# Decoder with causal self-attention on one core: the projections of a slot run ahead of a visit's transpositions instead of behind them

## The chip, the core and the metric

The kernel runs on one core of a Trainium2 chip. A core has TensorE (matmuls and transposes, results in PSUM), VectorE, ScalarE and GpSimd, which work on SBUF, and SyncE, which issues the DMAs here. Each engine takes its own instructions in order; semaphores tie them together. In the profile they are PE (with PEld for its weight loads), DVE, ACT, POOL and SP. The metric is the device time of one execution in microseconds: median 2737.55 us of three runs before the change (2737.44 to 2737.64).

## The reference

A small encoder works on a context of 2 x 77 rows of 512 numbers, and a decoder on 2 x 2048 rows of 512, everything in float32, 16 heads of 32. The part that matters here is the decoder's causal self-attention:

```python
yn = _ln(y, dec_n1_s, dec_n1_b)
q = yn @ wq.T + bq;  k = yn @ wk.T + bk;  v = yn @ wv.T + bv     # 16 heads of 32
scores = einsum('bhqd,bhkd->bhqk', q, k) / sqrt(32) + rel_bias + causal
out = einsum('bhqk,bhkd->bhqd', softmax(scores), v)
y = y + out @ w_out.T + b_out
y = y + _mha(_ln(y, dec_n2_s, dec_n2_b), memory, ...)            # 77 keys of the encoder
y = y + relu(_ln(y, ...) @ ff1.T + b1) @ ff2.T + b2
```

The relative bias is constant beyond a distance of 128, so that only the last two blocks of 128 keys of a row of blocks need a table added; the others need none, after the table has been shifted by its constant.

## The kernel before, in words

The self-attention is cut into units (b, m, g, t): batch b of 2, block m of 512 rows (4 of them), group g of four heads (4), tile t of 128 query rows (4). There are 128 units, taken in this order. Unit (b, m, g, t) attends to i + 1 blocks of 128 keys, with i = 4 m + t. The key blocks are cut into pieces of up to four (`pieces`), and one round of the main loop (a visit) handles up to two pieces of a unit. Blocks m = 0 and m = 1 have one visit per unit, m = 2 and m = 3 two: the last visit of a unit is the one with `ends` true.

A unit goes through these steps. `scores` (L375): for each piece four matmuls on TensorE, one head each, into four PSUM banks; VectorE takes them to the SBUF buffer `pp` and keeps the maxima (L384 for the far blocks, L391 for the last two with their table), and after the last piece forms the negated maximum (L401). Four exponentials on ScalarE (L406, one for each head, held in the list `late_exps` and issued by `exps`) work in place in `pp`. `turn` (L426): each 128 x 128 block is transposed by TensorE, four transposes to a bank, and each bank is copied to one of eight buffers `pts`, by ScalarE (L433) or VectorE (L431). For m = 0 a bank holds the blocks of one head and the two engines alternate; for m > 0 a bank holds one key block of the four heads and the first half of the copies is ScalarE's, the later half VectorE's (with eight banks VectorE has the fifth and the seventh). `turn` issues one exponential after its fourth bank (after the eighth of eight) and up to four at its end. `values` (L455): values times transposed probabilities, four heads at a time, into one bank, which is copied to `oT` (L466, L468, L470).

Scores run two units ahead: `may_score` lets a piece of unit n be scored as soon as unit n - 2 has turned the blocks that lie in the same part of `pp`.

PSUM has eight banks, handed out in turn by `bank()` from the list `ring`; a bank is used again after seven others, and its next matmul waits until the copy out of it has been made. `values` takes a bank out of the ring while it sums.

Beside the units there is a `slot` for each: stages of other work, put down by hand in three lists by number of slot. `light` stages come first (normalising rows of later blocks with `norm_turn`, L305 and L310; dividing by the sums with `spread`; loads of bias tables; cross-attention of an earlier block), then the jobs with weights: `q_job` (L215), `k_job` (L226), `v_job` (L239) for the next blocks, the seven-product `part_job` (L1068), each with one or two banks and a copy out of it by VectorE or ScalarE. The `late` stages follow, among them the stages of the encoder (L577 to L820, its scores at L606 with VectorE work at L615 and L616). Slot n + 1 is issued in the last visit of unit n.

After the units a second part computes cross-attention and feed-forward for the remaining blocks; the change does not touch it. The schedule is by hand: each engine runs its instructions in the order in which the program calls them.

Of the kernel before, what the change touches and what calls it, by code (L numbers as in the profile page):

```python
# [54 lines left out]
def tile_encoder_decoder(ctx: ExitStack, tc: tile.TileContext, ins, out):  # L55
# [103 lines left out]
    with (  # L159
# [20 lines left out]
        def bank():  # L180

            ring.append(ring.pop(0))
            return psum[:, ring[-1], :]

        def in_turn(what, tile):
            i = count[what] % tile.shape[1]
            count[what] += 1
            return tile[:, i, :]
# [140 lines left out]
        units = [(b, m, g, t) for b in range(B) for m in range(NMB) for g in range(NC) for t in range(TB)]  # L329
# [22 lines left out]
        def exps(k):  # L352

            for _ in range(min(k, len(late_exps))):
                late_exps.pop(0)[1]()
# [56 lines left out]
        def turn(pieces):  # L412

            first = units[pieces[0][0]][1] == 0
            loads = []
            for n, k0, kn in pieces:
                ks = range(k0, k0 + kn)
                if first:
                    loads += [[(n, k, r) for k in ks] for r in range(HC)]
                else:  # L420
                    loads += [[(n, k, r) for r in range(HC)] for k in ks]
            for o, load in enumerate(loads):
                pt = bank()
                pts = in_turn("pts", pts_all).rearrange("p (x q) -> p x q", q=P)
                for x, (n, k, r) in enumerate(load):
                    nc.tensor.transpose(pt[:, ts(x, P)], state[n]["p"][r][:, k], ident)  # L426
                    got[n, k, r] = pts[:, x, :]
                w = len(load) * P
                free = pieces[0][0] == len(units) - 2 and pieces[0][1]
                if free or (o % 2 if first else o in (4, 6) if len(loads) == 8 else o >= (len(loads) + 1) // 2):  # L430
                    nc.vector.tensor_copy(pts[:, : len(load), :], pt[:, :w])  # L431
                else:
                    nc.scalar.copy(pts[:, : len(load), :], pt[:, :w])  # L433
                if not first and o == (7 if len(loads) == 8 else min(3, len(loads) - 1)):
                    exps(1)
            exps(HC if first else 0 if units[pieces[0][0]][1] == NMB - 1 else 1)
# [3 lines left out]
        def values(pair):  # L440
            n, k0, _ = pair[0]
            b, m, g, t = units[n]
            i = m * TB + t
            k1 = pair[-1][1] + pair[-1][2]
            whole = m == 0
            key = (b, m, g) if whole else n
            begun = key in sums_held
            if not begun:
                sums_held[key] = ring.pop(0)
            v = sums_held[key]  # L450
            ot = psum[:, v, ts(t, P)] if whole else psum[:, v, :P]
            keep = t < TB - 1 if whole else (g, t) == (2, 0) and k1 <= i
            for k in range(k0, k1):
                for r in range(HC):
                    nc.tensor.matmul(  # L455
                        ot[rows4(r)], vv[:, k, ts(g * HC + r, HD)], got.pop((n, k, r)),
                        start=k == k0 and (whole or not begun), stop=k == k1 - 1 and (whole or not keep),
                    )
            if keep:
                return  # L460
            if (b, m, g) not in ots:
                ots_at[b, m, g] = count["oT"] % oT_all.shape[1]
                ots[b, m, g] = in_turn("oT", oT_all)
            o = ots[b, m, g]
            if whole:
                nc.scalar.copy(o, psum[:, v, :])  # L466
            elif k0 == 0 or begun:
                nc.scalar.copy(o[:, ts(t, P)], ot)  # L468
            else:
                nc.vector.tensor_tensor(o[:, ts(t, P)], ot, o[:, ts(t, P)], ALU.add)  # L470
            ring.append(sums_held.pop(key))
# [644 lines left out]
        for x, (b, m) in enumerate(blocks):  # L1116
# [28 lines left out]
            for t in range(TB):  # L1145
                end = x == len(blocks) - 1
# [44 lines left out]
        def load_next():  # L1191

            while len(loaded) < min(len(queue), ran[0] + (5 if ran[0] < 4 else 4)):
                ahead = [queue[i][2] for i in range(ran[0], len(loaded) + 1)]
                if sum(ahead) > 3:
                    break
                loaded.append(queue[len(loaded)][0]())
# [45 lines left out]
        def slot(n):  # L1243
            for f in light[n]:
                f()
            for _, run, _ in jobs[n]:
                load_next()
                run(loaded[ran[0]])
                ran[0] += 1
            for f in late[n]:  # L1250
                f()
            if n == 5:
                load_next()
# [205 lines left out]
        def feed(upto):  # L1459
            while fed[0] < upto:  # L1460
                src = next(tiles, None)
                if src is None:
                    return
                dst = w_ring[fed[0] % len(w_ring)]
                fed[0] += 1
                if len(src.shape) == 3:
                    dst = dst.rearrange("p (c o) -> p c o", c=2)
                nc.sync.dma_start(dst, src)
# [302 lines left out]
        end = len(units)  # L1771
# [3 lines left out]
        def may_score():  # L1775

            if at[0] == len(stream):
                return False
            n, k0, kn = stream[at[0]]
            if n < 2:  # L1780
                return True
            moved = TB * max(0, units[n - 2][1] - units[n][1]) if n % 2 else 0
            return turned_to[n - 2] >= min(k0 + kn + moved, size[n - 2])

        def score_next():
            n, k0, kn = stream[at[0]]
            scores(n, k0, kn)
            scored_to[n] = k0 + kn
            at[0] += 1

        def score_two():

            n, k0, kn = stream[at[0]]
            at[0] += 1
            both = may_score()
            at[0] -= 1
            if both and stream[at[0] + 1][0] == n and stream[at[0] + 1][2] < kn:
                scores(*stream[at[0] + 1])
                scores(n, k0, kn)
                scored_to[n] = size[n]  # L1800
                at[0] += 2
            else:
                score_next()
                if both:
                    score_next()
# [5 lines left out]
        while i < len(stream):  # L1811
            n = stream[i][0]
            pair = [p for p in stream[i : i + 2] if p[0] == n]
            while scored_to.get(n) != size[n]:
                score_next()
            while any(u == n for u, _ in late_exps):
                exps(1)
            ends = pair[-1][1] + pair[-1][2] == size[n]
            turn(pair)
            if n == end - 2:  # L1820
                for _, k0, _ in pair:
                    feed(k0 + 4)
            turned_to[n] = pair[-1][1] + pair[-1][2]
            third = units[n][1] == 2
            if third and ends:
                exps(2)
            if ends and n + 1 < end:
                slot(n + 1)
            if not third:
                exps((0, 2, 1, 1)[units[n][1]])  # L1830
            if may_score():
                if len(pair) > 1 and units[n][1]:
                    score_two()
                else:
                    score_next()
            values(pair)
            while may_score() and (len(pair) > 1 or units[n][1] == 0):
                score_next()
            if third and not ends:
                exps(2)  # L1840
            i += len(pair)
# [68 lines left out]
```

## Time and profile before

| what | value |
|---|---|
| median of three runs | 2737.55 us |
| the profiled execution: own time, span | 2739.13 us, 2737.3 us |
| PE busy | 2711.1 us (99%) |
| DVE busy | 1821.8 us (67%) |
| ACT busy | 1539.9 us (56%) |
| POOL busy | 991.1 us (36%) |
| L426, transposes of probabilities, on PE | 527.6 us, 4352 instructions |
| L375, scores, on PE | 331.7 us, 2560 instructions |
| L455, values, on PE | 278.8 us, 8704 instructions |
| L431, copies of transposed blocks by DVE | 251.6 us, 404 instructions |
| L433, the same by ACT | 383.6 us, 732 instructions |

A row of the timeline gives start and duration in us from the span's start, engine, line, operation, written and read buffers, shape and the number of instructions that were merged into it; in brackets stands the idle time before it and what ended it. Score and value matmuls are recorded twice each, so a scored piece shows eight records. Ends of matmuls are modelled, so that the distance between starts says more than the durations. The units run from about 28 us to 1663 us of the span.

### The profile page before, as it was taken

The page shows a single profiled execution, that of the slowest core. Times are in us where ns is not written, and L with a number is a line of the kernel's source. Part 1 is how long each engine was busy: PE and PEld are TensorE (multiplying, and loading weights), DVE is VectorE, ACT ScalarE, POOL GpSimd, SP SyncE. Part 2 cuts the span into 40 slices and gives each one's busy share as a digit, 9 for nine tenths or more (in the row PEclk, how much of TensorE's full clock was granted, in tenths as well). Part 3 has the DMA queues.
Part 4 walks back from the last instruction along what each step waited for, and adds up shares of the span by engine and source line. Part 5 has one row for each costly group of instructions (what it writes and reads, how often), then busy time and mean ns, then how long its engine had stood idle before and what let it go on. Part 6 is the DMA issues. An engine that isn't in the chain of part 4 may idle for free.

```text
span 2737.3 us, 67718 instructions
## 1 busy us (share of the span) xinstructions
PE 2711.1 (99%) x26462; PEld 2182.6 (80%) x26462; DVE 1821.8 (67%) x5338; ACT 1539.9 (56%) x2996; POOL 991.1 (36%) x836
## 2 busy tenths in 40 slices
PE   9999999999999999999999999999999999999998
PEld 5578777777776677777777887898989898989898
DVE  5776687787875587687787793646464746464645
ACT  3554567767786557667777785444444444444431
POOL 1512234500210513313300103465646564646456
PEclk9999999999999999999999999999999999999999
DMA  7624345511212522333311206565758565756465
GB/s 225 182 86 133 121 126 176 161 55 41 63 48 72 147 75 71 108 111 106 128 44 33 64 19 225 166 220 166 219 166 242 165 219 166 220 166 220 150 224 185
DMA packets 293666, 377.47 MB, mean 138 GB/s; under 512 B 39984, under 2 KB 163936, under 8 KB 293218
## 3 DMA queue, kind: packets, MB, share of 16 engines
q1 hardware_dynamic: 293346, 373.12, 44.3%
q8 instruction: 210, 3.44, 0.5%
q14 instruction: 110, 0.90, 0.1%
HBM read 328.38 MB, written 44.64 MB: 136 GB/s over the span
## 4 chain that ended last, share of the span: by engine, by line
PE 94%; ACT 2%; DVE 2%; issue 1%; POOL 0%; DMA 0%; SPq 0%; ACTq 0%; DVEq 0%; POOLq 0%
PE psum L426 18%; PE psum L1556 14%; PE psum L1585 12%; PE psum L375 11%; PE psum L455 9%; PE psum L1068 8%; PE psum L215 4%; PE psum L1719 3%; PE psum L1676 3%; PE psum L865 2%; ACT pp L406 1%; PE psum L835 1%; PE psum L873 1%; PE psum L589 1%; PE psum L810 1%; PE psum L239 1%
## 5 line engine op out<-in xcount | busy, mean ns | idle before, releaser
L406 ACT ACTIVATE pp<-pp,nm 128x128 f32<-128x128 f32 (+15 forms) x512 | 611.9, 1201 | 30.1 <-DVE nm L401 29.6
L384 DVE TENSOR_SCALAR_CACHE_REDUCE pp<-psum 128x512 f32<-128x512 f32 (+3 forms) x1024 | 556.4, 591 | 56.2 <-PE psum L375 53.7
L433 ACT COPY pts<-psum 128x512 f32<-128x512 f32 (+2 forms) x732 | 383.6, 580 | 277.0 <-PE psum L426 224.8
L426 PE MATMUL psum<-ident,pp 128*128 128x128 f32 x4352 | 527.6, 276 | 9.7 <-ACT nT L310 4.5
L426 PEld LDWEIGHTS psum<-ident,pp 128*128 128x128 f32 x4352 | 471.4, 140 | 67.1 <-DVE pp L384 24.0
L375 PE MATMUL psum<-kT,q 32*128 32x512 f32 (+3 forms) x2560 | 331.7, 560 | 2.8 <-ACT nT L310 1.6
L455 PEld LDWEIGHTS psum<-pts,vv 128*32 128x32 f32 x8704 | 226.6, 110 | 126.5 <-DVE pp L384 47.0
L431 DVE COPY pts<-psum 128x512 f32<-128x512 f32 (+3 forms) x404 | 251.6, 654 | 94.5 <-PE psum L426 92.5
L1585 PE MATMUL psum<-pp 128*128 128x128 f32 x2560 | 304.5, 276 | 1.9 <-POOL pp L961 1.6
L1585 PEld LDWEIGHTS psum<-pp 128*128 128x128 f32 x2560 | 296.3, 192 | 8.6 <-issue 3.0
L455 PE MATMUL psum<-pts,vv 128*32 128x128 f32 x8704 | 278.8, 275 | 0.7 <-DVE mx L391 0.3
L961 POOL TENSOR_TENSOR pp<-pp 128x512 f32<-128x512 f32 x159 | 212.9, 1356 | 121.0 <-DMA pp<-in_dec_ff_wT_dram 45.4
L1556 PE MATMUL psum<-vv,pp 128*128 128x256 f32 x1024 | 236.2, 381 | 0.0
L375 PEld LDWEIGHTS psum<-kT,q 32*128 32x128 f32 x2560 | 142.1, 183 | 106.7 <-issue 42.0
L1556 PEld LDWEIGHTS psum<-vv,pp 128*128 128x128 f32 x1024 | 190.3, 190 | 25.8 <-issue 0.5
L391 DVE CUSTOM_DVE_ANT_0 pp<-psum,bias 128x256 f32<-128x256 f32 (+1 forms) x512 | 196.0, 411 | 20.9 <-PE psum L375 20.8
L1569 DVE TENSOR_TENSOR kT<-kT,psum 128x512 f32<-128x512 f32 x96 | 65.8, 686 | 191.1 <-PE psum L1556 190.9
L1572 ACT ACTIVATE kT<-kT,vecs 128x256 f32<-128x256 f32 x192 | 87.1, 501 | 156.6 <-DVE kT L1569 155.9
L1556 PE MATMUL psum<-nT,pp 128*128 128x256 f32 x768 | 174.1, 380 | 0.0
L1556 PEld LDWEIGHTS psum<-nT,pp 128*128 128x128 f32 x768 | 144.2, 190 | 20.3 <-issue 1.6
L1593 ACT COPY oT<-psum 128x128 f32<-128x128 f32 x56 | 15.0, 268 | 238.8 <-PE psum L1585 238.8
L493 POOL TENSOR_TENSOR oT<-rirows,oT 128x512 f32<-128x512 f32 x30 | 38.4, 1279 | 288.5 <-DMA rirows<-rec 239.9
(257 smaller groups left out, 4049.3 us busy)
## 6 DMA issues: line engine op xcount, KB each, us to landing
pp<-w_d SPq DMA_DIRECT2D x520, 256.0 KB
pp<-in_dec_ff_wT_dram SPq DMA_DIRECT2D x112, 256.0 KB
wqk<-in_dec_sa_in_wT_dram SPq DMA_DIRECT2D x76, 256.0 KB
bias<-tzg SPq DMA_DIRECT2D x128, 128.0 KB
pp<-wo_d SPq DMA_DIRECT2D x56, 256.0 KB
vv<-in_enc_ff_wT_dram SPq DMA_DIRECT2D x8, 1024.0 KB
xr<-in_x_dram SPq DMA_DIRECT2D x32, 256.0 KB
vv<-y SPq DMA_DIRECT2D x32, 256.0 KB
```

Source lines behind the costliest of these rows:

```text
L375: nc.tensor.matmul(banks[r][:, : kn * P], q[rows4(r), ts(t, P)], kT[rows4(r), g, k0 * P : (k0 + kn) * P], start=True, stop=True,)
L384: nc.vector.tensor_scalar(p[:, k0 : k0 + far], s[:, :far], 1.0, None, ALU.mult, ALU.max, accum_out=st["mx"][:, r, c : c + 1],)
L391: nc.vector.tensor_tensor_reduce(p[:, k0 + far : i + 1], s[:, far:kn], near[:, 2 - (kn - far) :], 1.0, LOWEST, ALU.add, ALU.max, accum_out ...
L406: nc.scalar.activation(p, p, AF.Exp, bias=nm, accum_out=to)
L426: nc.tensor.transpose(pt[:, ts(x, P)], state[n]["p"][r][:, k], ident)
L431: nc.vector.tensor_copy(pts[:, : len(load), :], pt[:, :w])
L433: nc.scalar.copy(pts[:, : len(load), :], pt[:, :w])
L455: nc.tensor.matmul(ot[rows4(r)], vv[:, k, ts(g * HC + r, HD)], got.pop((n, k, r)), start=k == k0 and (whole or not begun), stop=k == k1 - ...
L961: engine.tensor_tensor(out, a, b, ALU.subtract)
L1068: nc.tensor.matmul(mm[:, ts(f, TOK)], left[:, c, ts(f, P)], right[:, c, :], start=c == 0, stop=c == 1,)
L1556: nc.tensor.matmul(mm[:, ts(f, TOK)], a[:, c, ts(f, P)], b[:, c, :], start=fresh and f == 0 and c == 0, stop=c == 1, skip_group_check=True,)
L1585: nc.tensor.matmul(psum[:, bank_i, ts(col, P)], lhs[:, c, :], w[:, c, :], start=fresh and k in (0, 3) and c == 0, stop=c == 3, skip_group_ ...
```

## The change

The call of `slot(n + 1)` in a unit's last visit moves from behind `turn` to ahead of it, and with it, for m = 2, the issue of up to two exponentials. The order in a last visit was: transpose, slot, scores, values. It is now: slot, transpose, scores, values. So a slot's work stands between the values of the visit before and the transpositions. Nothing is added or left out. Visits that do not end a unit stay as they are.

```diff
             ends = pair[-1][1] + pair[-1][2] == size[n]
+            third = units[n][1] == 2
+            if ends and n + 1 < end:
+                if third:
+                    exps(2)
+                slot(n + 1)
             turn(pair)
             if n == end - 2:
                 for _, k0, _ in pair:
                     feed(k0 + 4)
             turned_to[n] = pair[-1][1] + pair[-1][2]
-            third = units[n][1] == 2
-            if third and ends:
-                exps(2)
-            if ends and n + 1 < end:
-                slot(n + 1)
             if not third:
                 exps((0, 2, 1, 1)[units[n][1]])
             if may_score():
```

## The prediction

> **What bounds the kernel now.** I read the page's busy shares and chain of waits first, then TensorE's timeline visit by visit, then VectorE's and ScalarE's timelines beside it. The page settles the engine.
>
> ```profile
> PE 2711.1 (99%) x26462; PEld 2182.6 (80%) x26462; DVE 1821.8 (67%) x5338; ACT 1539.9 (56%) x2996; POOL 991.1 (36%) x836
> PE 94%; ACT 2%; DVE 2%; issue 1%; POOL 0%; DMA 0%; SPq 0%; ACTq 0%; DVEq 0%; POOLq 0%
> ```
>
> TensorE is at work for 2711.1 of 2737.3 us and carries 94% of the chain. Its work is not changed by the edit: the same matmuls run in another order. So the time can move only through stalls of TensorE, and many of these are hidden in "busy", because the ends of matmuls are modelled. I take a stall as the distance from the start of one group to the start of the next, less the same distance where nothing stalls. In this way four kinds of group are told apart in a visit: T (transposes of probabilities, L426), J (the slot's jobs, here L215), S (scores, L375) and V (values, L455).
>
> The first fence is TensorE's timeline in the last quarter of a batch (m = 3), two units whose last visit has a slot with one projection. The second is the same part of two later units whose slot holds no matmul, so that S follows T at once, which is what the change makes of every last visit.
>
> ```profile
> 619.17 2.84 PE L426 MATMUL psum<-ident,pp 128*128 128x128 f32 x24
> 621.84 3.60 PE L215 MATMUL psum<-nT,wqk 128*128 128x512 f32 x8
> 625.37 2.03 PE L375 MATMUL psum<-kT,q 32*128 32x512 f32 x16
> 627.34 1.52 PE L455 MATMUL psum<-pts,vv 128*32 128x128 f32 x48
> 628.78 4.18 PE L426 MATMUL psum<-ident,pp 128*128 128x128 f32 x32
> 632.90 2.00 PE L375 MATMUL psum<-kT,q 32*128 32x512 f32 x16
> ...
> 672.63 2.40 PE L426 MATMUL psum<-ident,pp 128*128 128x128 f32 x20
> 674.87 3.60 PE L215 MATMUL psum<-nT,wqk 128*128 128x512 f32 x8
> 678.40 2.04 PE L375 MATMUL psum<-kT,q 32*128 32x384 f32 x16
> 680.36 1.30 PE L455 MATMUL psum<-pts,vv 128*32 128x128 f32 x40
> ...
> 685.24 1.14 PE L375 MATMUL psum<-kT,q 32*128 32x512 f32 x8
> ```
>
> ```profile
> 812.16 2.40 PE L426 MATMUL psum<-ident,pp 128*128 128x128 f32 x20
> ...
> 821.66 2.00 PE L375 MATMUL psum<-kT,q 32*128 32x512 f32 x16
> ...
> 825.48 2.84 PE L426 MATMUL psum<-ident,pp 128*128 128x128 f32 x24
> 828.25 2.53 PE L375 MATMUL psum<-kT,q 32*128 32x512 f32 x16
> 830.70 1.52 PE L455 MATMUL psum<-pts,vv 128*32 128x128 f32 x48
> 832.15 3.79 PE L426 MATMUL psum<-ident,pp 128*128 128x128 f32 x32
> 835.87 0.50 PE L375 MATMUL psum<-kT,q 32*128 32x128 f32 x8
> ```
>
> The reader is to see two things. A projection costs 3.53 us (621.84 to 625.37) wherever it stands. And S straight behind T takes 2.45 us (828.25 to 830.70) against 1.97 (625.37 to 627.34) behind a projection: 0.48 more. But the next T is then quicker, 3.72 (832.15 to 835.87) against 4.12 (628.78 to 632.90), so most of it comes back.
>
> **The change part by part.** *The order on TensorE.* In a unit's last visit T, J, S, V becomes J, T, S, V. Of the 128 units 127 have such a slot. Each sequence has the same matmuls, so the first cost is nothing; what covers the copies of T's banks to SBUF changes. Before, J runs while VectorE and ScalarE empty the banks; after, S must be given banks that T has just filled, and V must read the last copy, with S alone between. What is queued behind a waiting S is all of TensorE: V, the next J, the next T.
>
> *Price of S behind T, blocks m = 1 and 3.* From the first T of the last visit to the S of the next visit, less the slot's 3.53: 632.90 - 619.17 - 3.53 = 10.20 with a slot and 835.87 - 825.48 = 10.39 without, +0.19; for the 20 transposes 685.24 - 672.63 - 3.53 = 9.08 and 821.66 - 812.16 = 9.50, +0.42. The cause is on VectorE, in the same stretch:
>
> ```profile
> 827.10 0.69 DVE L384 TENSOR_SCALAR_CACHE_REDUCE pp<-psum 128x512 f32<-128x512 f32 x1
> 827.72 1.88 DVE L431 COPY pts<-psum 128x512 f32<-128x512 f32 x3
> ```
>
> VectorE still empties the scores of the visit before when T ends its fourth load, and its three copies finish at 829.60, 4.12 us after T began. With J ahead of T it has had 3.53 us more and is through. The fourth load (16 of 24 transposes, 2.77 x 16/24 = 1.85 us after T's start) then starts the copies at once: they finish 1.85 + 1.88 = 3.73 us after T's start, 0.39 earlier. So I take 0.1 us a visit, half of the smaller price, with bounds 0 and 0.42. It applies to 49 visits: 30 of the 32 of m = 1 and 19 of the 32 of m = 3 have matmul work for a microsecond or two in their slot. 49 x 0.1 = +5 us, bounds 0 and +21.
>
> *m = 2.* The last visit turns two to four blocks (one to two VectorE copies) and scores one piece into four banks that T did not use. No such wait is to be seen; 0. The two exponentials that the edit puts ahead of the slot find an empty list, since the visit before has issued all four.
>
> *Slots with hardly any matmul.* In eight last visits of m = 1, 2, 3 the slot is a normalised tile's four transposes, alone or with a short stage of cross-attention.
>
> ```profile
> 747.63 0.60 PE L305 MATMUL psum<-ident,xt 128*128 128x128 f32 x4
> 748.16 1.93 PE L375 MATMUL psum<-kT,q 32*128 32x384 f32 x12
> 750.92 1.13 PE L375 MATMUL psum<-kT,q 32*128 32x512 f32 x4 [0.83 <-ACT nT L310]
> 751.98 1.30 PE L455 MATMUL psum<-pts,vv 128*32 128x128 f32 x40
> ```
>
> ```profile
> 747.57 1.81 ACT L406 ACTIVATE pp<-pp,nm 128x1792 f32<-128x1792 f32 x1
> 749.35 1.51 ACT L310 ACTIVATE nT<-psum,vecs 128x128 f32<-128x128 f32 x4
> ```
>
> S takes 3.82 here (748.16 to 751.98) instead of 1.96 (678.40 to 680.36), since its last bank is the slot's, which ScalarE empties behind T's copies and an exponential. After the change the slot's four activations come first on ScalarE, ahead of T's copies. If all eight lose this 1.86 now, 15 us could be had. But those activations then delay T's copies and both exponentials by 1.51, and ScalarE has no less to do; I take half, -7, bounds -15 and 0.
>
> *m = 0.* A visit here is short, and VectorE copies T's second and fourth bank.
>
> ```profile
> 81.56 0.52 PE L426 MATMUL psum<-ident,pp 128*128 128x128 f32 x3 [0.57 <-ACT pts L433]
> 82.15 3.70 PE L226 MATMUL psum<-nT,wqk 128*128 128x512 f32 x8
> ...
> 87.26 0.50 PE L375 MATMUL psum<-kT,q 32*128 32x128 f32 x8 [0.69 <-ACT kT L231]
> 87.69 0.86 PE L455 MATMUL psum<-pts,vv 128*32 128x128 f32 x24
> ```
>
> ```profile
> 77.63 1.63 DVE L615 TENSOR_TENSOR pp<-psum,pp 77x308 f32<-77x308 f32 x4
> 79.29 1.43 DVE L616 TENSOR_REDUCE emx<-pp 77x16 f32<-77x1232 f32 x1
> ...
> 83.59 1.01 DVE L431 COPY pts<-psum 128x384 f32<-128x384 f32 x2
> ```
>
> ```profile
> 108.20 1.20 PE L426 MATMUL psum<-ident,pp 128*128 128x128 f32 x9 [1.41 <-ACT nT L310]
> ...
> 113.90 1.53 PE L426 MATMUL psum<-ident,pp 128*128 128x128 f32 x12 [1.81 <-ACT nT L310]
> ```
>
> With 12 or 16 transposes S lasts 0.43 (87.26 to 87.69) or little more, and one VectorE copy is 1.01 / 2 = 0.51: V now waits some 0.25 us in the 16 visits with t of 2 or 3, +4. The encoder's scores hold VectorE from 77.63 to 80.72. Before, J's 3.7 us at 82.15 hide that T's copies come only at 83.59; after, in the two slots with encoder scores, T's copies stand right behind 3.1 us of this work, while T and S last 1.4 + 0.43: about 2 us of wait each, +4, less the waits of 0.57 and 0.69 and a long S that stand there now, so +2. Against it: T waits 1.41 and 1.81 for a bank that the slot before filled; a slot directly ahead of T, and S and V between the next pair, shift this; half of it, and as much for waits of T on VectorE behind the last scores, which then have a projection's time: -3.5. m = 0 together +2.5, bounds -3 and +8.
>
> *Other queues.* GpSimd's instructions keep their order. SyncE's differ in one place, the last unit: three loads go ahead of ten weight tiles for the feed-forward part.
>
> ```profile
> 1412.00:1663.00 251.00, 249.78 (x3356) 197.42 (x3356) 200.13 (x654) 196.52 (x293) 22.59 (x18) 1.00 0.19 61
> ```
>
> The last column but one is the share of the DMA engines, 0.19 there, with matmuls of several microseconds between issue and use: 0. Were the cover gone, one tile's delay would cost a wait of its landing at most once. Elsewhere each slot's loads are issued one T (2 to 3.6 us) sooner, to the same distance of a unit or more from their use: 0.
>
> *Sum.* +5 + 0 - 7 + 2.5 = +0.5 us. The profiled execution took 2739.13 us (span 2737.3 and 1.8 around it), so it would be 2739.6; the median of the runs was 2737.55, 1.6 below that execution, so I forecast 2738.0.
>
> **The rivals.** *Faster.* The slots' short visits recover all 15 us, T's waits in m = 0 go (-3) and S behind T costs nothing, as J has cleared VectorE: -18, 2720. For it speaks that the no-slot rows above pay back most of S's delay in the next T; against it, that ScalarE's amount of work in those visits is the same.
>
> *Slower, by banks.* S waits in each of the 49 visits for T's last copy, as where no slot stands between now: 0.42 each, +21, with no gain in the short slots: 2758. It decides from 0.25 us a visit on, if the other terms stand as taken (49 x 0.25 = 12, less 4.5, is over 0.2%). A projection's own copy on VectorE standing ahead of T's would bring it; against it stands that VectorE copies only from the fourth load on. [...]
>
> *Slower, by exponentials.* In m = 3 the last two exponentials of the next unit stand behind T's copies; J now no longer lies before the next T.
>
> ```profile
> 827.65 1.92 ACT L406 ACTIVATE pp<-pp,nm 128x1920 f32<-128x1920 f32 x1
> 829.54 1.90 ACT L406 ACTIVATE pp<-pp,nm 128x1920 f32<-128x1920 f32 x1
> ```
>
> They end at 831.44, and the next T begins at 832.15: a margin of 0.7 us. Were ScalarE 1.7 us later in each of the 32 units, T would wait 1 us in each: +32, 2770.
>
> **How the numbers follow.** No change, about 2738: 0.40. Faster rival: 0.28. Slower by banks: 0.28; by exponentials: 0.04. The bounds of all terms together are -18 and +29; I leave out the ends of both and take 2723 to 2757; the likeliest case alone spans 2732 to 2743. About 0.2% (5.5 us) is what a measurement of this kernel can tell from no change, so faster 0.28, same 0.40, slower 0.32.
>
> **What would show it.** In TensorE's timeline of m = 3, S behind T near 2.1 to 2.4 us and T behind the next V near 3.6 to 3.7; in the short slots S down from 3.82 to under 3; in m = 0 a wait of V for VectorE's copies (L431), about 2 us in the two slots of encoder scores; granted clock unchanged at 1.00. The forecast is wrong if S or V wait over half a microsecond in most last visits, or if the short slots give all back.

## The result, and the profile after

The changed kernel takes 2765.12 us (median of 4 runs, 2761.89 to 2767.87) where the kernel before took 2737.60 on the same chip: a ratio of 1.0099, with a 95% interval of 1.0087 to 1.0111. It is 27.5 us slower. The forecast was 2738.0 with a range of 2723 to 2757, so the time lies beyond the range's upper end.

First the page of the profile after: the busy shares, then the chain of work by engine.

```profile
PE 2729.5 (99%) x26462; PEld 2210.5 (80%) x26462; DVE 1826.2 (66%) x5338; ACT 1537.9 (56%) x2996; POOL 990.9 (36%) x836
...
PE 93%; ACT 3%; DVE 2%; DMA 1%; issue 1%; POOL 0%; SPq 0%; DVEq 0%; ACTq 0%; POOLq 0%
```

TensorE has the same 26462 instructions and is "busy" 18.4 us longer (2729.5 against 2711.1), while the span grew by 28.8 us (2766.1 against 2737.3). Since no work was added, both are waits of TensorE or work at a slower clock. ScalarE's share of the chain is up from 2% to 3%, both rounded, one per cent of 2766 being 27.7 us. The view of TensorE's waits names what is new: line waiting, what it waits for, then total us, number of waits, the longest.

```profile
PE psum L455 <- ACT pts L433: 8.8, 4, 2.9
PE psum L426 <- ACT pp L406: 8.1, 6, 1.4
```

Before, no value matmul waited for a ScalarE copy of transposed probabilities at all (that row is not there), and the second row stood at 1.9 us in 3 waits. These two are 8.8 and 8.1 us now. In return T's waits for L310 (4.5 us in 4 waits before, of which 1.41 and 1.81 stood in m = 0 and twice 0.63 behind the short slots of m = 2) are gone.

Where the time went follows from cutting the span at the start of the group behind the last values of each block m. I write the difference after less before, in us:

| block | m = 0 | m = 1 | m = 2 | m = 3 |
|---|---|---|---|---|
| batch 0 | +4.9 | -0.2 | +5.6 | +6.6 |
| batch 1 | +5.3 | -4.6 | +4.9 | +6.3 |

The sum, 28.8, is the whole growth of the span: the second part of the program begins 28.7 us later (L1556 first at 1691.98 instead of 1663.25) and is not changed. Two entries are not the edit's alone. Of the first 4.9, 0.7 lie ahead of the first scores (24.4 us instead of 23.7), where both kernels run the same program. And of the -4.6, 1.6 are a stretch of half clock that the profiled execution of before had there, as the run with the short slots will show.

A second thing is new. The table of stretches of the profile after (start:end, length, busy us of PE, PEld, DVE, ACT and POOL, then the granted clock, and the DMA engines' share and GB/s) has six stretches of 3.4 us in the units' part in which TensorE's clock is half. They begin at 517.5, 626.7, 981.7, 1005.6, 1346.9 and 1456.1 us; the first:

```profile
517.50:520.90 3.40, 3.40 (x18) 3.40 (x18) 0.29 (x1) 1.76 (x3) 2.34 (x3) 0.50 0.38 132
```

Before there was one, from 1108.4 to 1111.8 us. By my estimate from these numbers, 3.4 x (1 - 0.50), up to 1.7 us of work are lost in such a stretch; five more stretches are up to 8.5 of the 28.8 us. The mean clock of the span is 0.996 against 0.999.

Units are numbered below as in the runs' expectations: n = 64 b + 16 m + 4 g + t, so 32 to 47 are m = 2 of the first batch, and "the values of visit 41" are those of unit 41's last visit. T, J, S and V are the four kinds of group from the prediction, and a stall is again the distance of starts less the same distance where nothing stalls.

**m = 2, short slots (units 40 and 41, 104 and 105).** TensorE's waits and ScalarE's timeline of the kernel after:

```profile
500.71 0.64 PE L455 MATMUL psum<-pts,vv 128*32 128x128 f32 x16 [1.50 <-ACT pts L433]
...
511.83 1.46 ACT L406 ACTIVATE pp<-pp,nm 128x1408 f32<-128x1408 f32 x1
...
513.28 1.46 ACT L406 ACTIVATE pp<-pp,nm 128x1408 f32<-128x1408 f32 x1
...
514.73 1.48 ACT L310 ACTIVATE nT<-psum,vecs 128x128 f32<-128x128 f32 x4
...
516.11 0.58 ACT L433 COPY pts<-psum 128x512 f32<-128x512 f32 x1
...
516.74 0.64 PE L455 MATMUL psum<-pts,vv 128*32 128x128 f32 x16 [2.90 <-ACT pts L433]
```

The same place before:

```profile
505.17 0.56 ACT L433 COPY pts<-psum 128x512 f32<-128x512 f32 x1
...
505.63 1.47 ACT L406 ACTIVATE pp<-pp,nm 128x1408 f32<-128x1408 f32 x1
...
507.10 1.46 ACT L406 ACTIVATE pp<-pp,nm 128x1408 f32<-128x1408 f32 x1
...
507.11 0.64 PE L455 MATMUL psum<-pts,vv 128*32 128x128 f32 x16
...
508.55 1.49 ACT L310 ACTIVATE nT<-psum,vecs 128x128 f32<-128x128 f32 x4
```

Here lies the largest misreading. T fills two banks in this visit; VectorE copies the second, ScalarE the first. Before, ScalarE's copy (505.17) came ahead of two exponentials (505.63, 507.10) and of the slot's activations (508.55); the values at 507.11 did not wait, and the exponentials ran beside V and the next T. After, exponentials and the slot's activations stand in a row (the last two exponentials and L310: 511.83 to 516.11) ahead of the copy, and the values wait 2.90 us; the first of the six stretches of half clock (0.50) follows at 517.5. In visit 40 the slot's activations alone cost 1.50 (500.71).

**m = 3, first units (48 and 49, 112 and 113).** After, then before:

```profile
618.62 1.81 ACT L406 ACTIVATE pp<-pp,nm 128x1792 f32<-128x1792 f32 x1
...
622.07 0.60 PE L426 MATMUL psum<-ident,pp 128*128 128x128 f32 x2
...
623.95 1.78 ACT L406 ACTIVATE pp<-pp,nm 128x1792 f32<-128x1792 f32 x1
...
624.11 0.33 PE L426 MATMUL psum<-ident,pp 128*128 128x128 f32 x1 [1.44 <-ACT pp L406]
...
625.88 5.05 PE L426 MATMUL psum<-ident,pp 128*128 128x128 f32 x29 [1.44 <-ACT pp L406]
...
630.86 2.00 PE L375 MATMUL psum<-kT,q 32*128 32x512 f32 x16
```

```profile
604.84 1.89 PE L1068 MATMUL psum<-wqk,xr 128*128 128x256 f32 x8
...
611.52 3.90 PE L426 MATMUL psum<-ident,pp 128*128 128x128 f32 x32
...
615.35 1.14 PE L375 MATMUL psum<-kT,q 32*128 32x512 f32 x8
```

Four exponentials of 1.8 us of unit 49 stand between T(48) and T(49) in both kernels. Before, a projection (two groups from 604.84 to 608.39) ran beside the first ones, and T(49) took 3.83 us (611.52 to 615.35). After, the first stands at 618.62 and the last at 623.95, the projection is over before T(48), and T(49) waits twice 1.44 us for its third and fourth exponential and then runs at half clock (0.50 from 626.7 to 630.1): 8.79 us from 622.07 to 630.86.

**m = 0.** VectorE and TensorE in unit 6 of the kernel after:

```profile
90.28 1.43 DVE L616 TENSOR_REDUCE emx<-pp 77x16 f32<-77x1232 f32 x1
...
91.45 0.48 PE L375 MATMUL psum<-kT,q 32*128 32x128 f32 x2 [0.67 <-ACT pts L433]
...
91.63 1.01 DVE L431 COPY pts<-psum 128x384 f32<-128x384 f32 x2
```

The encoder's additions and maxima (the last of them L616, here) hold VectorE until 91.63, and only then are T's second and fourth bank copied; the score at 91.45 waits 0.67 for ScalarE's copy of T's first bank. In m = 0 the sum of the values keeps one of the eight banks, so seven go round, and S's fourth bank is T's first.

### The profile page after: what moved, and what is told of

Read it like the earlier page. It is cut to its first block, busy times and chain, and to the rows that moved or that the text cites. A ratio compares the mean times of both kernels' runs of the same rounds, so it can differ in the third digit from the quotient of the medians.

```text
span 2766.1 us, 67812 instructions
## 1 busy us (share of the span) xinstructions
PE 2729.5 (99%) x26462; PEld 2210.5 (80%) x26462; DVE 1826.2 (66%) x5338; ACT 1537.9 (56%) x2996; POOL 990.9 (36%) x836
## 4 chain that ended last, share of the span: by engine, by line
PE 93%; ACT 3%; DVE 2%; DMA 1%; issue 1%; POOL 0%; SPq 0%; DVEq 0%; ACTq 0%; POOLq 0%
PE psum L426 17%; PE psum L1556 14%; PE psum L1585 12%; PE psum L375 11%; PE psum L455 9%; PE psum L1068 8%; PE psum L215 4%; PE psum L1719 3%; PE psum L1676 3%; PE psum L865 2%; ACT pp L406 2%; PE psum L873 1%; PE psum L835 1%; PE psum L810 1%; PE psum L589 1%; PE psum L239 1%
## 5 line engine op out<-in xcount | busy, mean ns | idle before, releaser
L426 PE MATMUL psum<-ident,pp 128*128 128x128 f32 x4352 | 521.0, 276 | 8.6 <-ACT pp L406 8.1
L426 PEld LDWEIGHTS psum<-ident,pp 128*128 128x128 f32 x4352 | 486.4, 142 | 52.1 <-issue 28.6
L375 PE MATMUL psum<-kT,q 32*128 32x512 f32 (+3 forms) x2560 | 343.5, 562 | 4.3 <-ACT pts L433 1.3
L455 PE MATMUL psum<-pts,vv 128*32 128x128 f32 x8704 | 284.7, 275 | 10.7 <-ACT pts L433 8.8
L1556 PE MATMUL psum<-vv,pp 128*128 128x256 f32 x1024 | 236.2, 381 | 0.0
L375 PEld LDWEIGHTS psum<-kT,q 32*128 32x128 f32 x2560 | 152.7, 183 | 81.2 <-DVE pts L431 19.0
L1556 PEld LDWEIGHTS psum<-vv,pp 128*128 128x128 f32 x1024 | 190.3, 190 | 25.8 <-issue 0.5
L1556 PE MATMUL psum<-nT,pp 128*128 128x256 f32 x768 | 174.1, 380 | 0.0
L1556 PEld LDWEIGHTS psum<-nT,pp 128*128 128x128 f32 x768 | 144.2, 190 | 20.3 <-issue 1.6
```

Of the source, the lines that this page charges most:

```text
L375: nc.tensor.matmul(banks[r][:, : kn * P], q[rows4(r), ts(t, P)], kT[rows4(r), g, k0 * P : (k0 + kn) * P], start=True, stop=True,)
L455: nc.tensor.matmul(ot[rows4(r)], vv[:, k, ts(g * HC + r, HD)], got.pop((n, k, r)), start=k == k0 and (whole or not begun), stop=k == k1 - ...
L1556: nc.tensor.matmul(mm[:, ts(f, TOK)], a[:, c, ts(f, P)], b[:, c, :], start=fresh and f == 0 and c == 0, stop=c == 1, skip_group_check=True,)
```

## The experiments

**The change in one block number at a time.** Four kernels make the edit only where the unit's m is X; the other last visits keep the old order. Edits are shown against the changed kernel.

```diff
+            early = units[n][1] in (X,)
-            if ends and n + 1 < end:
+            if early and ends and n + 1 < end:
                 if third:
                     exps(2)
                 slot(n + 1)
             turn(pair)
...
+            if not early:
+                if third and ends:
+                    exps(2)
+                if ends and n + 1 < end:
+                    slot(n + 1)
```

> Only the last visits of blocks m = 0 have the slot ahead of the transposes. Theory A (the loss comes in a few kinds of visit whose copies of T stand late: short visits of m = 0, short slots of m = 2, the first unit of m = 3; plus stretches of halved clock that follow long waits): the two blocks m = 0 lost 4.9 + 5.3 = 10 us in the changed kernel's trace, two halved stretches among it, so +5 to +10 us. Theory B (every last visit pays alike for S straight behind T): 27.5 us over 127 visits is 0.22 a visit, 32 visits, +7 us.

> Only blocks m = 1. Theory A: these two blocks gained in the changed kernel (0.2 and 4.6 us), so -3 to -5 us against the kernel before. Theory B: +7 us as for each of the four blocks.

> Only blocks m = 2. Theory A: the loss sits in two visits of each batch whose slot is a normalised tile alone, where V waits for ScalarE's copy behind four activations and two exponentials; 5.6 + 4.9 us in the trace, one halved stretch in each; +7 to +11 us. Theory B: +7 us spread over the 32 last visits.

> Only blocks m = 3. Theory A: 6.6 + 6.3 us in the trace, most in the visit behind the first unit of the block, where four exponentials stand between T and the next T (two waits of 1.44 us and a halved stretch); +8 to +13 us. Theory B: +7 us spread evenly.

| edit in | median us | ratio to before (2737.59) | 95% interval |
|---|---|---|---|
| m = 0 | 2747.25 | 1.0038 | 1.0023 to 1.0052 |
| m = 1 | 2735.53 | 0.9993 | 0.9984 to 1.0002 |
| m = 2 | 2750.81 | 1.0050 | 1.0035 to 1.0065 |
| m = 3 | 2750.67 | 1.0050 | 1.0035 to 1.0065 |

The differences of the medians are +9.7, -2.1, +13.2 and +13.1; their sum, 33.9, is 6.4 above the 27.5 of the whole change. The loss is not spread over the visits: m = 1, with 32 moved slots, loses nothing. In the traces m = 2 loses in visits 37, 40 and 41 of each batch (0.8, 1.4 and 3.4 us), m = 3 in 49 and 63 of the first batch (5.5 and 1.7) and in 113 of the second (5.2), m = 0 in a dozen visits by up to 1.7 us each (in unit 75 by 2.9, of which 1.2 return in unit 76), against waits of T that go. Two of these traces are not like their medians: that of m = 0 took 2744.27 us, 3 less than the median, and that of m = 2 has four stretches of half clock, two of them (at 114.5 and 759.6 us) in places where nothing was edited (granted clock 0.57 from 114 to 117 us; mean clock of this execution 0.997). The theory that each last visit pays alike is refuted. What an ordinary visit does is seen in TensorE's timeline of the kernel with the edit in m = 3 alone:

```profile
648.64 2.08 PE L375 MATMUL psum<-kT,q 32*128 32x256 f32 x16
...
650.65 1.74 PE L455 MATMUL psum<-pts,vv 128*32 128x128 f32 x56
...
652.32 3.71 PE L426 MATMUL psum<-ident,pp 128*128 128x128 f32 x32
...
655.96 2.00 PE L375 MATMUL psum<-kT,q 32*128 32x512 f32 x16
```

S behind T takes 2.01 us (648.64 to 650.65), hardly more than behind a projection before (1.97), and the next T takes 3.64 (652.32 to 655.96), as little as without a slot (3.72).

**m = 3 with the exponentials ahead of the slot.** In m = 3 the edit stays, and all exponentials in the list but the last two (in units 62 and 126 all of them) are issued ahead of the slot, beside J (the lines for the late order as above).

```diff
+            early = units[n][1] == 3
+            if early and ends and n + 1 < end:
                 if third:
                     exps(2)
+                if units[n][1] == 3:
+                    exps(len(late_exps) - (0 if units[n][2:] == (3, 2) else 2))
                 slot(n + 1)
```

> The edit is made in the block m = 3 alone, and there all exponentials of the next unit that would stand between two transposes are issued ahead of the slot, where the slot's projection hides them. Edit in m = 3 alone cost 13 us. Theory A (ScalarE's exponentials between the transposes of visits 48 and 49 and of 62 and 63, in each batch, no longer covered by a projection, and the halved clock behind such waits): the transposes of visit 49 go back from 8.6 to about 3.8 us, those of 63 from 5.2 to 3.7, no stretch of halved clock is left, and the time is 2738 to 2743. Theory B (scores straight behind transposes cost the same in each last visit): the exponentials' place does not matter, and the time stays at 2750.

2740.70 us, ratio 1.0014 (1.0004 to 1.0023): 10 us of the 13 come back. Its timeline at unit 49:

```profile
610.28 1.79 ACT L406 ACTIVATE pp<-pp,nm 128x1792 f32<-128x1792 f32 x1
...
611.95 3.71 PE L426 MATMUL psum<-ident,pp 128*128 128x128 f32 x32
```

The last of the four exponentials now starts at 610.28, before T(49) at 611.95, and T(49) no longer waits; no stretch of half clock is left in the units' part (granted clock 1.00 from 612 to 618 us, where it is 0.51 from 615 to 618 with the edit in m = 3 alone; mean clock 1.0). What remains sits in unit 62, where the exponentials are now too early for T's copies instead (T 1.9 and V 0.8 us longer): a wait displaced by the repair.

**m = 2 without the short slots.** The edit in m = 2 only ahead of slots with a job (`early = units[n][1] == 2 and jobs[n + 1]`).

> The edit is made in the block m = 2 alone, and there only ahead of slots that hold a projection or another job; the slots that hold only a normalised tile stay where they were. Edit in m = 2 alone cost 13 us. Theory A (the loss sits in the visits 37, 40 and 41 of each batch, where the normalised tile's activations stand ahead of the last copy of the probabilities): 2736 to 2740, and no halved clock near 514 and 1336 us. Theory B (each last visit loses alike): 29 of the 32 slots are still moved, so 2749.

2740.56 us, ratio 1.0014 (1.0004 to 1.0023). Of the 13 us 10 are gone, with the waits of visits 40 and 41 and the half clock behind them (mean clock of the profiled execution 1.0 instead of 0.997). This is half a microsecond above the expected range: visit 37, whose slot holds a projection, keeps its 0.8 us, and I had counted it with the short slots.

**m = 2, which of ScalarE's instructions.** The slot goes ahead of T, the two exponentials stay behind T.

```diff
-            if ends and n + 1 < end:
-                if third:
-                    exps(2)
+            if third and ends and n + 1 < end:
                 slot(n + 1)
             turn(pair)
...
+            if third and ends:
+                exps(2)
+            elif ends and n + 1 < end:
+                slot(n + 1)
```

> As the edit in m = 2 alone, but the two exponentials of the last visit stay behind the transposes, where they were; only the slot goes ahead. In visit 41 of each batch the last copy of the probabilities stands behind two exponentials of 1.5 us and the slot's activations of 1.5 us. Theory A (the prediction's step that the list of exponentials is empty there was wrong, and these two make the wait of 2.9 us and the halved clock behind it): the values of visit 41 wait less than 0.3 us, no halved clock follows, the wait of 1.5 us in visit 40 stays, and the time falls from 2751 to 2741 to 2745. Theory B (the slot's activations alone make the wait): the values of visit 41 still wait 1.4 us or more, and the time is 2747 or above.

2751.12 us, ratio 1.0049 (1.0032 to 1.0066), no gain over the edit in m = 2. The mechanism is theory A's and the time theory B's, and the trace says why. TensorE and ScalarE at unit 41, and the row of the waits:

```profile
510.58 0.65 PE L455 MATMUL psum<-pts,vv 128*32 128x128 f32 x16
...
511.87 1.48 ACT L406 ACTIVATE pp<-pp,nm 128x1408 f32<-128x1408 f32 x1
...
513.49 3.38 PE L426 MATMUL psum<-ident,pp 128*128 128x128 f32 x29 [1.12 <-ACT pp L406]
```

```profile
PE psum L426 <- ACT pp L406: 11.9, 13, 1.1
```

The values of visit 41 (510.58) wait for nothing now and no half clock follows (mean clock 1.0), as theory A had it. But the exponential at 511.87, behind T, makes T(42) wait, and this is so in other units too: T(34), T(38) and T(46) are 1.3, 0.8 and 1.3 us longer than before, and so are their like in the second batch. T waits 11.9 us for exponentials in 13 places, where before it waited 1.9. The two exponentials of the last visit exist ahead of these units, and they need J to run beside: ahead of J they are hidden except in the short slot (and in part in visit 37), behind T they are not. In visit 40, where the list is empty, the wait of 1.5 us stays: there the slot's activations alone make it, and in visit 41 it takes the exponentials.

**m = 2 with the gap filled.** The edit in m = 2, and in visit 41 of each batch 28 transposes of the identity are put on TensorE ahead of the values; their results are overwritten.

```diff
+            if (m, g, t) == (2, 2, 1) and k1 == i + 1:
+                for _ in range(28):
+                    nc.tensor.transpose(psum[:, v, :P], ident, ident)
```

> As the edit in m = 2 alone, with 28 transposes of the identity added on TensorE in visit 41 of each batch, ahead of the value matmuls that wait there; their results are overwritten and not used. Theory A (the halved clock follows TensorE's idle time in this visit): the stretches of 3.4 us at clock 0.5 near 514 and 1336 us go, and the time falls from 2751 by about 2 x 1.7 = 3.4 us, less what the added transposes take beyond the wait, to 2747 to 2749. Theory B (the clock falls for another reason): the stretches stay and the time is 2751 or above.

TensorE's timeline and the stretch 514 to 517 us, first with the edit in m = 2 alone, then with the gap filled:

```profile
514.01 1.08 PE L455 MATMUL psum<-pts,vv 128*32 128x128 f32 x16 [2.90 <-ACT pts L433]
...
515.02 4.76 PE L426 MATMUL psum<-ident,pp 128*128 128x128 f32 x32
...
519.72 1.87 PE L375 MATMUL psum<-kT,q 32*128 32x384 f32 x16
```

```profile
514.00:517.00 3.00, 2.99 (x26) 2.58 (x27) 0.39 (x2) 0.59 (x1) 2.47 (x3) 0.50 0.28 106
```

```profile
509.39 3.28 PE L455 MATMUL psum<-ident 128*128 128x128 f32 x28
...
512.59 0.65 PE L458 MATMUL psum<-pts,vv 128*32 128x128 f32 x16
...
513.17 3.71 PE L426 MATMUL psum<-ident,pp 128*128 128x128 f32 x32
...
516.81 1.87 PE L375 MATMUL psum<-kT,q 32*128 32x384 f32 x16
```

```profile
514.00:517.00 3.00, 3.00 (x31) 2.83 (x33) 1.15 (x2) 2.64 (x6) 2.92 (x4) 1.00 0.03 5
```

From V to the next S it is 5.71 us unfilled (514.01 to 519.72) and 4.22 filled (512.59 to 516.81): the stretch of half clock cost 1.49 us here, and it is gone where the added transposes fill the wait (clock 1.00 instead of 0.50 from 514 to 517 us). The kernel's time is 2747.35 us, ratio 1.0039 (1.0024 to 1.0054), against 1.0050 (1.0035 to 1.0065): as expected in size. But the intervals overlap, and the stretches of the unfilled run at 114.5 and 759.6 us, where nothing was filled, are missing in this one too, so the price of a stretch rests on the trace.

**m = 0 with the late stages behind.** The edit in m = 0; of a slot only the light stages and the jobs go ahead of T (second argument 0), the late stages (the encoder, argument 1) stay behind it.

```diff
+                slot(n + 1, 0)
             turn(pair)
...
+            if early and ends and n + 1 < end:
+                slot(n + 1, 1)
```

> The edit is made in the block m = 0 alone, and of a slot only the normalised tiles and the projections go ahead of the transposes; the late stages (scores of the encoder and what follows on them) stay behind them. Edit in m = 0 alone cost 9.7 us. Theory A (values wait because the encoder's stages on VectorE stand ahead of the copies of the probabilities in a few visits): the waits of visits 5 to 8 shrink, and the time is 2740 to 2744. Theory B (each last visit of m = 0 loses since scores and values follow the transposes too soon): it stays at 2746 to 2749.

2740.80 us, ratio 1.0012 (1.0002 to 1.0022), of 9.7 us 3.1 are left. Unit 6 with the whole slot ahead, then with the late stages behind:

```profile
90.92 1.30 PE L455 MATMUL psum<-pts,vv 128*32 128x128 f32 x22 [0.84 <-DVE pts L431]
```

```profile
85.30 1.33 PE L375 MATMUL psum<-kT,q 32*128 32x128 f32 x8 [1.12 <-DVE pts L431]
```

The wait of the values for VectorE's copies (0.84) is gone. The encoder's scores now stand between T and S, and S waits 1.12 for the same copies there. In sum over the first batch's m = 0, counted from the first scores, stalls are 0.6 us below the kernel before instead of 4.1 above; in the second batch they are 3.5 above instead of 2.8. In both batches there is a stretch of half clock among them (105.4 and 986.0 us), which the run with the whole slot ahead does not have (mean clock 0.999 here, 1.0 there).

**Only the short slots of m = 1 and m = 3.** `early = units[n][1] in (1, 3) and not jobs[n + 1]`.

> The edit is made only in last visits of m = 1 and m = 3 whose slot holds no projection (24, 56, 57, 88, 89 and the last eight of the second batch). Theory A (a slot with hardly any matmul is better ahead of the transposes, since there its bank is emptied before the scores need it; all the rest of the edit is neutral or a loss): the gains of the visits 57, 88 and 89, which were 1.2, 2.7 and 1.7 us, come alone, and the time is 2731 to 2734. Theory B (those gains were other waits displaced by the moves around them): 2736 to 2739.

2735.95 us, ratio 0.9994 (0.9985 to 1.0003): at the lower edge of theory B's range and 2 us above theory A's. The traces say why. Unit 88 before, then in this kernel, then in the kernel with the edit in m = 3 alone, which leaves this slot where it was:

```profile
1104.32 4.05 PE L375 MATMUL psum<-kT,q 32*128 32x384 f32 x16
...
1108.30 2.32 PE L455 MATMUL psum<-pts,vv 128*32 128x128 f32 x40
...
1110.54 3.44 PE L426 MATMUL psum<-ident,pp 128*128 128x128 f32 x24
```

```profile
1105.00 2.23 PE L375 MATMUL psum<-kT,q 32*128 32x384 f32 x16
...
1107.16 1.30 PE L455 MATMUL psum<-pts,vv 128*32 128x128 f32 x40
```

```profile
1111.36 4.05 PE L375 MATMUL psum<-kT,q 32*128 32x384 f32 x16
...
1115.34 1.30 PE L455 MATMUL psum<-pts,vv 128*32 128x128 f32 x40
```

The stretch of before that covers V, as above (length, busy us of the engines, clock):

```profile
1108.40:1111.80 3.40, 3.40 (x46) 3.02 (x46) 1.78 (x7) 1.00 (x4) 0.00 (x0) 0.50 0.89 251
```

Before, S took 3.98 and V 2.24 us (1104.32, 1108.30, 1110.54), V at half clock; now S takes 2.16 (1105.00 to 1107.16). So the slot's place is worth 1.82 us here. The rest is the clock: with the slot in its old place S takes 3.98 again (1111.36 to 1115.34), but V runs 1.30 instead of 2.32, and in all eight other runs that leave the slots of units 88 and 89 alone these units are 1.6 us shorter than in the profiled execution of before, with its stretch of half clock from 1108.4. Of the 4.4 us that units 88 and 89 gain against that execution, 2.8 are the edit's. 57 gains 1.2, but T(90) is 0.9 longer and T(11) in m = 0, where nothing was edited, met a stretch of half clock in this profiled execution (0.60 from 114 to 117 us).

**Nine slots.** The edit only in the visits where a single block's trace showed a gain: `early = n in (9, 10, 16, 17, 56, 57, 70, 88, 89)`.

> The edit is made in nine last visits alone, which are those where the runs with the edit in one block showed a gain: 9, 10 and 70 of m = 0, 16, 17, 88 and 89 of m = 1, 56 and 57 of m = 3. Theory A (the edit's effect is local to a visit and the next one): the gains add, 5.8 for the four slots without a projection, 1.6 for 16 and 17, 1.2 for 70 and 1.2 for 9 and 10, and the time is 2727 to 2731, faster than both kernels. Theory B (waits only move from one visit to another): 2735 or more.

2731.58 us (10 runs, 2730.15 to 2734.25), ratio 0.9978 (0.9969 to 0.9987): 6.0 us faster than the kernel before and 33.5 faster than the changed one. That is 0.6 us beyond the expected range and short of the sum of gains, 9.8. Of the 5.8 expected of the four short slots 1.6 were the clock, as just said, and T(90) is again 0.9 longer. Units 9 to 11 gain 1.3 as expected, but 16 and 17 only 0.8, since a projection of slot 17 now waits 0.63 for its weights, and 69 and 70 nothing: the transposes of slot 71, now earlier, wait for GpSimd's rows.

```profile
903.25 0.66 PE L305 MATMUL psum<-ident,xt 128*128 128x128 f32 x4 [1.23 <-POOL xt L293]
```

TensorE is busy 5 us less than before (2706.1) with the same 26462 instructions, 1.6 of it the stretch of half clock.

**All blocks, without the four causes.** Late stages behind T in m = 0; in m = 2 and 3 the short slots and those of visits 37, 48 and 62 of each batch as before; all else moved.

```diff
+            early = units[n][1] < 2 or jobs[n + 1] and n not in (37, 48, 62, 101, 112, 126)
```

> The edit in all blocks, less what the earlier runs named as its costs: in m = 0 the late stages stay behind the transposes, in m = 2 and 3 the slots without a projection stay where they were, and so do those of the visits 37, 48 and 62 of each batch. Theory A (four local causes and the halved clock behind them are the whole loss of 27.5 us): the sums of the single blocks give +3, -2, +3 and +1, so 2739 to 2745. Theory B (part of the loss comes only when all blocks are moved, or each last visit pays a little): 2752 or more.

2741.48 us, ratio 1.0012 (1.0003 to 1.0021). Of the 27.5 us 3.9 are left, while most of the slots are still moved. So 23.6 us of the loss are local, and these places hold them. In this run's trace, cut as in the first table, the largest loss left is 6.1 us in m = 0 of the second batch, with stretches of half clock of 6.8 and 3.4 us (from 962.75 and 990.05; mean clock 0.998).

## Why the prediction was wrong

The step that failed is the path through ScalarE. The sum followed what TensorE and VectorE had to do and took ScalarE's queue at nothing in m = 2 (0, measured +13.2) and for m = 3 put it into a rival with a chance of 0.04 (measured +13.1, almost all of it T's waits for exponentials and the clock behind them). Part by part:

*What bounds the kernel.* Right: instructions are the same, and all but 0.7 us of the difference arises in the units' part, in waits of TensorE and its slower clock.

*S behind T in m = 1 and 3, +0.1 a visit.* Right in size. In m = 3, over the 17 moved visits with a job other than 49, 63 and 113, the stalls sum to +1.7 us, 0.1 each. In m = 1 of the first batch S became 2.0 us longer in sum and T 1.8 shorter, as the prediction had read it. The rival "by banks", at 0.42 a visit, is refuted by the same numbers, though its total (2758) was nearer than the forecast's.

*m = 2, "the two exponentials find an empty list".* This step failed. In its old place behind `turn`, the call finds an empty list indeed. But in ten of the 32 last visits (units 33, 37, 41, 45, 47 and the same of the second batch) the order of the program's calls leaves two exponentials in the list when the visit begins; `turn` issued them, behind its copies, just before. ScalarE's timeline of before shows a copy with two exponentials behind it in these ten (505.17, 505.63 and 507.10 for unit 41). Moved ahead of `turn`, the call finds them, and they go ahead of the slot and the copies. The prediction carried what held in the old place over to the new one. Its "no such wait is to be seen" was about waits of S on T's banks; the one that came is V's wait for ScalarE's copy. Taken as 0, measured +13.2, which includes the short slots' share.

*Short slots, -7.* The mechanism was named in both directions: the slot's activations go ahead of S's bank, and they delay T's copies. In m = 1 and m = 3 the first decides (-2.8 in units 88 and 89 without the clock, -1.4 in 56 and 57), in m = 2 the second (+1.4 in unit 40 of each batch; the +3.4 of unit 41 needs the exponentials too, as the run with these behind T shows). One sign for all eight was the mistake. I take T's length to be the difference between m = 2 and the others, which no run here tested: T has 8 transposes in that visit of m = 2 (about 1 us, less than the 1.5 us of activations ahead of its copy), and 20 or 24 in units 88 and 89.

*m = 0, +2.5.* The direction of each term was right and the sizes were not: +9.7 (interval 6 to 14), the median above the bound of 8. In the first batch of the run with m = 0 alone T's distances fell by 6.1 us (taken: 3.5 in both batches), V's rose by 5.2, and S's rose by 6.2, which the sum did not hold: S's last bank is T's first, as the row at 91.45 shows.

*The rival by exponentials, 2770 with a chance of 0.04.* In m = 3 this mechanism was the one that mattered, in another shape. I had read the margin at a pair of ordinary units (0.7 us) and asked what happens if all 32 slip; in fact the ordinary ones hold, and units 49 and 113, with four exponentials behind one T, wait for two of them. The margin had to be read at the worst unit. With J ahead of T nothing of TensorE's lies between the exponentials and the next T but S and V.

*Granted clock unchanged at 1.00.* Wrong, and the sum had no term for it: six stretches instead of one, up to 8.5 us. Its condition was read from a profiled execution of before that itself had one, at 1108.4.

*Other queues.* Nearly as taken: in the profile after one projection waits 0.50 us for its weights (974.11), and one wait of 0.81 of before is gone. With fewer slots moved such waits came up to 0.95 us (the run with m = 0 alone).

What stays open: why the short slots of m = 2 lose where the others gain; 3.1 us of m = 0; and the four runs with one block each sum to 6.4 us more than the whole change, and which stretches of half clock come differs from execution to execution, so I can't divide the 27.5 us more finely than into the named places.

## What to carry to other kernels

When independent work is moved from behind a step to ahead of it, list for every engine what ran beside it: here a projection hid ScalarE's exponentials and the copies, and the loss came in the few visits where the queue was longest, not in the average one. Read margins at the worst instance of each kind (first unit of a block, shortest slot, shortest transposition), and check whether a list that is empty in the old place is empty in the new one. And such a move need not be made everywhere: in nine of 127 places it gained 6 us, in all of them it lost 27.5.

## What the runs showed of the hardware

In these runs waits of TensorE of 2.90 us and less were followed by 3.4 us at half clock. In the changed kernel a wait of 2.90 us stands ahead of one stretch (517.5), two of 1.44 ahead of another (626.7), and, as far as the records show waits, two of 0.51 and 0.72 (1002.99 and 1004.62) ahead of a third (1005.6); the granted clock is 0.50 in all three. Behind the wait of 2.90 us of the run with m = 2 alone the stretch cost another 1.49, as measured above. The length of a wait alone did not decide here. The prediction's rows of before show T waiting 1.41 and 1.81 us at 108.20 and 113.90, with the clock at full (1.00 from 108 to 117 us). The same pair stands in the run with m = 2 alone and in the run with only the short slots moved, and there a stretch follows; in the latter the second T takes 2.55 us instead of 1.53:

```profile
108.60 1.20 PE L426 MATMUL psum<-ident,pp 128*128 128x128 f32 x9 [1.42 <-ACT nT L310]
...
114.30 2.55 PE L426 MATMUL psum<-ident,pp 128*128 128x128 f32 x12 [1.81 <-ACT nT L310]
```

The granted clock from 114 to 117 us is 0.60 in this run and 0.57 in the run with m = 2 alone. Why a stretch comes in one execution and not in another was not shown.
